# Three QR steps a tick, a QR tail in six places, and a shorter gap between the first two blocks

## The chip, the cores and the metric

The kernel runs on one core of a Trainium2 chip. The metric is the time on the device, in microseconds (us). The engines of a core work side by side, each through its own instructions in their order: TensorE (PE, with its weight loads PEld), VectorE (DVE), ScalarE (ACT), GpSimd (POOL) and SyncE (SP, which issues most of the DMAs).

## The reference

The input x has 32 sequences of 128 tokens with 144 channels. Four blocks follow each other, all conditioned on one vector a sequence. L0, L2 and L3 are transformer blocks with 16 heads of 9 channels; L0 normalises q and k, and L3 has four experts of which each token takes two. L1 is a rotation:

```python
U, _ = jnp.linalg.qr(P)                     # P: 144 x 64, one for all sequences
R = _rotation(cond, W, b)                   # expm of a skew 64 x 64 matrix a sequence
z = jnp.einsum('btn,nd->btd', x, U)
z_rot = jnp.einsum('btd,bde->bte', z, R)
x_rot = x + jnp.einsum('btd,nd->btn', z_rot - z, U)
```

Both the QR of P and the 32 matrix exponentials depend on the weights and the condition alone, not on x.

## The kernel before

All of x stays on the chip (`x_sb`). The three transformer blocks are called layers 0, 1 and 2 (L0, L2 and L3 of the reference). The kernel is one long loop over **ticks**. In a tick one sequence has its scores (`scores`, first half n = 0 and second half n = 1), the sequence before it has its scores once more, transposed, for the softmax weights, and the one before that has its attention output (`weigh`), its sums, its division and its projection. Sequence b of layer l begins at tick `first[l] + b`. Everything else is hung on to places of a tick. The places (called gaps in the code) are, in the order in which `fill` is called for them: a, e, t, first scores, stats, attention output, b0, b, den, (sums of layer 0), pre1, second scores, c, (division of layer 0), y1, y2, d, the largest scores, z. The instructions come out in exactly this order (`manual_schedule`), so each engine's queue is written out by hand: an instruction that waits holds up all that stand behind it on its engine. Banks of PSUM come from a pool of seven.

`GAP` is the number of ticks without a new sequence between layer 0 and layer 1: `first` is (0, 39, 71), so layer 0 has its scores in ticks 0 to 31 and layer 1 from tick 39. Layers 1 and 2 follow each other without a gap. The MLP of a group of four sequences of layer 0 is put 10 to 13 ticks behind the group's first tick; so groups 6 and 7 have theirs in ticks 34 to 41. The rotation of a group (`rotate_T`, `rotate_in`, `rotate`) is put 8 and 7 ticks ahead of the group's first tick in layer 1, and the layer norm and the q and k of layer 1 behind that.

Beside layer 0 the kernel prepares the rotation, by three generators that stop at each `yield`:

- `prep_qr`: 64 Householder steps of three pieces each (192 pieces, `qr_rest`), and then a tail of 18 pieces (a triangular inverse and U). In a step, piece one is a product on PE that spreads row j of `at` over all partitions (L322), ACT's square and its copy (L333, L335), and POOL's square root (L334). Piece two is five DVE instructions (L337 to L344), piece three two of them (L348, L349); the last one writes `at`, which the next step's product reads. The steps are one chain through four engines.
- `prep_expm`: 50 pieces: two layers' modulations and gates, the skew matrices (with two batches of weights by DMA), powers, two series, and four squarings in two pieces each. A squaring piece is 32 products of 64 x 64 on PE (L524) and two copies on ACT.
- `prep_rot`: eight pieces that make `rotU` out of U and the exponentials; behind it `load_late` frees the preparation's memory and loads the weights of layers 1 and 2.

`prepare_qr` gives out pieces of the QR: in ticks below 0 three a tick; from tick 0 six a tick, which is two steps (a: 1, t: 2, den: 1, y1: 1, y2: 1). When the steps are used up (tick 28), one piece of the tail is given out in every place of a tick, and then those of `prep_rot` in the same way: all in ticks 28 to 30. `prepare_expm` gives out one piece in b and one in z, up to tick 24. What is left at `last_prep` (tick 31, place d) is finished there; nothing is.

Of the kernel before, what the change touches and what calls it, by code (L numbers as in the profile page):

```python
# [65 lines left out]
def tile_kernel(ctx: ExitStack, tc: tile.TileContext, a: dict, out: bass.AP):  # L66
# [138 lines left out]
    def ring(shape, name, n, fill):  # L205
        bufs = []
        for i in range(n):
            t = const.tile(shape, F32, name=f"{name}{i}")
            fill(t)
            bufs.append(t)  # L210
        state = {"i": 0}

        def take():
            state["i"] += 1
            return bufs[(state["i"] - 1) % n]

        return take
# [93 lines left out]
    qr_rest = 3 * D  # L311
# [300 lines left out]
    def prep_rot(rotT):  # L612
        for b in range(0, NB2, 2):
            ps = bank([128, 2, C], f"ps_ru{b}")
            for i in range(2):
                for h in range(2):
                    rows = slice(h * D, (h + 1) * D)
                    nc.tensor.matmul(
                        ps[rows, i, :], rotT[rows, b + i, :], uT[rows, :], start=True, stop=True
                    )  # L620
            nc.scalar.copy(rotU[:, b : b + 2, :], ps)
            yield
# [10 lines left out]
    def ln_stats(pairs):  # L633

        n = len(pairs)
        name = "_".join(f"{kind}{s}" for s, kind in pairs)
        mv = small.tile([128, n, 2], F32, tag="mv", name=f"mv_{name}")
        for k, (s, kind) in reversed(list(enumerate(pairs))):
            bs = small.tile([128, 6], F32, tag="st", name=f"st_{kind}_{s}")
            nc.vector.bn_stats(bs, x_sb[:, of(s)[1], :])  # L640
            nc.vector.bn_aggr(mv[:, k, :], bs)  # L641
        rs = small.tile([128, 2, n], F32, tag="rs", name=f"rs_{name}")
        nc.gpsimd.tensor_scalar(rs[:, 0, :], mv[:, :, 1], 1.0, EPS, ALU.mult, ALU.add)  # L643
        nc.gpsimd.tensor_tensor(rs[:, 0, :], rs[:, 0, :], neghalf[:, :n], ALU.pow)
        nc.gpsimd.tensor_scalar(rs[:, 1, :], mv[:, :, 0], -1.0, 0.0, ALU.mult, ALU.add)
        for k, (s, kind) in enumerate(pairs):
            b = of(s)[1]
            minus, r = rs[:, 1, k : k + 1], rs[:, 0, k : k + 1]
            xh = work.tile([128, CM], F32, tag="xh", name=f"xh_{kind}_{s}", bufs=3)
            nc.gpsimd.tensor_scalar(xh, x_sb[:, b, :CM], minus, r, ALU.add, ALU.mult)  # L650
            xr = take_xr()
            nc.gpsimd.tensor_scalar(
                xr.rearrange("p (k c) -> p k c", k=4)[:, :, :CR],
                x_sb[:, b, CM:].unsqueeze(1).to_broadcast([128, 4, CR]),
                minus, r, ALU.add, ALU.mult,
            )
            st[s][f"xh_{kind}"], st[s][f"xr_{kind}"] = xh, xr
# [463 lines left out]
    late = L3 = None  # L1121
# [6 lines left out]
    def load_late():  # L1128
        nonlocal late, L3
        prep.close()  # L1130
        late = ctx.enter_context(tc.tile_pool(name="late", bufs=1))
        q = nc.sync
        PARAMS[1] = load_attn(late, "L2", q)
        load_mlp("L2", MLP_COLS)
        PARAMS[2] = L3 = Block()
        for k in ("wgate", "wgateR"):
            setattr(L3, k, load(late, f"L3_{k}", q))
        load_pair(0, late.tile([128, PAIR_COLS], F32, name="pair0"))
# [18 lines left out]
    prep_qr, prep_expm = prep_qr(), prep_expm()  # L1157
# [19 lines left out]
    def prepare_qr(tick, gap):  # L1177


        nonlocal prep_qr, prep_last, qr_rest  # L1180
        if late is not None:
            return
        if qr_rest:
            if tick < 0:
                pieces = {"e": 1, "stats": 2}
            else:

                pieces = {"a": 1, "t": 2, "den": 1, "y1": 1, "y2": 1}
            for _ in range(pieces.get(gap, 0)):
                next(prep_qr)  # L1190
                qr_rest -= 1
        elif prep_qr:
            if next(prep_qr, 0) == 0:
                prep_qr = None
        elif prep_last is None and not prep_expm:
            prep_last = prep_rot(rot_T[0])
        elif prep_last and next(prep_last, 0) == 0:
            load_late()

    def prepare_expm(tick, gap):  # L1200
        nonlocal prep_expm
        if prep_expm and (tick >= 0 and gap in ("b", "z") or (tick, gap) == (-2, "z")):
            said = next(prep_expm, 0)
            if said == 0:
                prep_expm = None
            elif said is not None:
                rot_T.append(said)


    GAP = 7  # L1210
    first = (0, B + GAP, 2 * B + GAP)
    at_tick = {first[l] + b: l * B + b for l in range(3) for b in range(B)}
    gaps = defaultdict(list)
    stats = defaultdict(list)
# [100 lines left out]

    def fill(tick, gap):
        prepare_qr(tick, gap)
        while (tick, gap) == (last_prep, "d") and late is None:
            prepare_qr(tick, gap)
            prepare_expm(tick, gap)  # L1320

        if gap == ("t" if tick < 0 else "e" if tick < first[1] else "stats") and tick in stats:
            ln_stats(stats.pop(tick))
        for f, args in gaps.pop((tick, gap), ()):
            f(*args)
        prepare_expm(tick, gap)

    last_prep = first[1] - 8
    for tick in range(-6, first[2] + B + 14):
        s0, s1, s2 = (at_tick.get(tick - k) for k in range(3))  # L1330
        for layer in range(3):
# [5 lines left out]
        while sums_later:  # L1337
            sums_later.pop()()
        fill(tick, "a")
        fill(tick, "e")  # L1340
        fill(tick, "t")
# [198 lines left out]
```

## Time and profile before

| what | us |
|---|---|
| median of 3 runs (lowest, highest) | 1370.38 (1369.37, 1375.61) |
| the profiled execution, its own time | 1370.79 |
| its span in the profile | 1368.0 |
| PE busy, PE's mean granted clock | 1296.2, 0.989 |
| start to tick 0's `q` (L822) | 51.1 |
| ticks 1 to 31 of layer 0 | 381.9 |
| ticks 32 to 39, between the layers | 46.2 |
| PE's idle time before QR products (L322), ended by DVE's `at` (L349) | 22.4, in 15 waits |

A tick is read here from one start of DVE's L822 (`q`) to the next, which occurs once a tick in which a sequence has its scores. "Busy" is the time in which at least one instruction of the engine was under way; PE's matmuls are pipelined and their ends are modelled. "x2 ... [1.91 <-DVE at L349]" behind a row says that the engine was idle for 1.91 us before it, and that DVE's write of `at` in line 349 ended the wait. PEclk is the share of its full clock that PE was granted.

### The profile page before, as it was taken

The page shows a single profiled execution, that of the slowest core. Times are in us where ns is not written, and L with a number is a line of the kernel's source. Part 1 is how long each engine was busy: PE and PEld are TensorE (multiplying, and loading weights), DVE is VectorE, ACT ScalarE, POOL GpSimd, SP SyncE. Part 2 cuts the span into 40 slices and gives each one's busy share as a digit, 9 for nine tenths or more (in the row PEclk, how much of TensorE's full clock was granted, in tenths as well). Part 3 has the DMA queues.
Part 4 walks back from the last instruction along what each step waited for, and adds up shares of the span by engine and source line. Part 5 has one row for each costly group of instructions (what it writes and reads, how often), then busy time and mean ns, then how long its engine had stood idle before and what let it go on. Part 6 is the DMA issues. An engine that isn't in the chain of part 4 may idle for free.

```text
span 1368.0 us, 35736 instructions
## 1 busy us (share of the span) xinstructions
PE 1296.2 (95%) x14210; PEld 951.4 (70%) x14210; DVE 825.7 (60%) x2632; ACT 812.3 (59%) x1800; POOL 639.6 (47%) x1663
## 2 busy tenths in 40 slices
PE   7999898999989988999999999999999999999998
PEld 5678687787767566677767676767676767676765
DVE  4698888866764357676666666646464545454322
ACT  2568776768746445776666767655555555554431
POOL 4667776655742523343443433626262626151622
PEclk9999999999999999999999999999999999999999
DMA  8200000000003000000110000200000000000000
GB/s 227 59 3 19 19 19 2 19 20 4 19 2 118 35 2 19 10 20 10 43 27 19 15 15 10 73 10 19 10 19 10 18 10 19 10 18 1 19 9 9
DMA packets 21608, 34.57 MB, mean 25 GB/s; under 512 B 2176, under 2 KB 12256, under 8 KB 21184
## 3 DMA queue, kind: packets, MB, share of 16 engines
q1 hardware_dynamic: 20848, 31.68, 7.8%
q8 instruction: 114, 1.87, 0.6%
q10 hardware_dynamic: 592, 0.59, 0.2%
q14 instruction: 54, 0.44, 0.1%
HBM read 29.79 MB, written 2.47 MB: 24 GB/s over the span
## 4 chain that ended last, share of the span: by engine, by line
PE 66%; DVE 8%; ACT 1%; issue 1%; POOLq 0%; POOL 0%; DVEq 0%
PE ps_h L682 19%; PE ps_f L1102 8%; PE ps_qk L682 6%; PE ps_s L858 5%; PE ps_o L885 5%; PE ps_w L858 5%; PE ps_f L975 4%; DVE nm L863 3%; PE ps_pj L949 3%; PE ps_v L682 2%; PE ps_f L1106 1%; PE ps_o L817 1%; DVE block L914 1%; DVE oT L916 1%; DVE block L910 1%
## 5 line engine op out<-in xcount | busy, mean ns | idle before, releaser
L863 DVE TENSOR_REDUCE nm<-ps_s 128x4 f32<-128x512 f32 x384 | 246.3, 682 | 88.1 <-PE ps_w L858 78.7
L870 ACT ACTIVATE pr<-ps_w 128x512 f32<-128x512 f32 x384 | 208.4, 595 | 143.6 <-PE ps_w L858 141.8
L858 PE MATMUL ps_w<-q,kT 32*128 32x128 f32 x3072 | 235.0, 284 | 1.6 <-DVE kT L736 1.6
L858 PE MATMUL ps_s<-kT,qT 32*128 32x256 f32 x1536 | 232.7, 408 | 0.1
L858 PEld LDWEIGHTS ps_w<-q,kT 32*128 32x128 f32 x3072 | 198.4, 188 | 13.3 <-issue 6.0
L969 ACT ACTIVATE hid<-ps_h 128x512 f32<-128x512 f32 (+1 forms) x224 | 119.3, 591 | 107.6 <-PE ps_h L682 107.3
L935 POOL TENSOR_TENSOR x_sb<-x_sb,res_a 128x144 f32<-128x144 f32 x96 | 46.9, 489 | 265.0 <-DVE res_a L938 264.4
L858 PEld LDWEIGHTS ps_s<-kT,qT 32*128 32x128 f32 x1536 | 136.3, 186 | 28.0 <-issue 9.0
L682 PE MATMUL ps_h<-hM_m,mlps 128*128 128x512 f32 x304 | 145.3, 611 | 0.0
L1110 DVE SCALAR_TENSOR_TENSOR acc<-ps_f,cw,acc 128x144 f32<-128x144 f32 x128 | 46.7, 366 | 158.6 <-PE ps_f L1106 72.3
L885 PE MATMUL ps_o<-pr,vaug 128*32 128x128 f32 x3072 | 105.0, 277 | 0.1
L885 PEld LDWEIGHTS ps_o<-pr,vaug 128*32 128x32 f32 x3072 | 78.8, 110 | 33.0 <-PE ps_w L858 18.5
L682 PEld LDWEIGHTS ps_h<-hM_m,mlps 128*128 128x128 f32 x304 | 54.2, 193 | 66.7 <-issue 65.8
L975 PE MATMUL ps_f<-mlps,hid 128*128 128x144 f32 x640 | 93.3, 293 | 0.0
L975 PEld LDWEIGHTS ps_f<-mlps,hid 128*128 128x128 f32 x640 | 82.4, 191 | 8.1 <-issue 5.1
L672 ACT ACTIVATE hM_m<-ps_hT_m,modM 128x128 f32<-128x128 f32 x96 | 44.6, 465 | 73.0 <-PE ps_hT_m L670 72.8
L643 POOL TENSOR_SCALAR rs_m_a<-mv_m_a 128x2 f32<-128x2 f32 x81 | 15.5, 191 | 137.2 <-DVE mv_m_a L641 109.7
L935 POOL TENSOR_TENSOR x_sb<-x_sb,res_m 128x144 f32<-128x144 f32 x64 | 32.6, 509 | 96.2 <-DVE res_m L938 96.2
L870 ACT ACT_TABLE_LOAD x55 | 70.6, 1283 | 5.6 <-PE ps_w L858 4.7
L1102 PEld LDWEIGHTS ps_f<-pair,hid 128*128 128x128 f32 x512 | 67.2, 191 | 8.4 <-issue 7.7
L1102 PEld LDWEIGHTS ps_f<-mlps,hid 128*128 128x128 f32 x512 | 67.2, 191 | 8.0 <-issue 6.9
L966 ACT ACT_TABLE_LOAD x56 | 71.8, 1283 | 1.0
(327 smaller groups left out, 2965.2 us busy)
## 6 DMA issues: line engine op xcount, KB each, us to landing
gates<-gates SPq DMA_DIRECT2D x48, 288.0 KB, 3.5
x_sb<-in_x SPq DMA_DIRECT2D x8, 288.0 KB, 8.7
out_x<-x_sb SPq DMA_DIRECT2D x8, 288.0 KB, 2.5
mlps<-in_L_mlp SPq DMA_DIRECT2D x2, 1000.0 KB, 6.7
wt<-in_W SPq DMA_DIRECT2D x6, 320.0 KB, 8.1
pair<-in_L_mlp SPq DMA_DIRECT2D x1, 1800.0 KB, 8.7
mlps<-in_L_mlp SPq DMA_DIRECT2D x1, 1800.0 KB, 8.5
mlps<-in_L_wmod SPq DMA_DIRECT2D x4, 290.0 KB, 4.7
```

The costliest lines, as they stand in the source:

```text
L672: nc.scalar.activation(gr[g][f"{k}_{kind}"][:, i, :], ps[:, k == "hR", :], AF.Identity, bias=m[:, sh, b : b + 1], scale=m[:, sc, b : b + 1],)
L682: nc.tensor.matmul(ps, x, y, start=k == 0, stop=k == 1)
L858: nc.tensor.matmul(o, x, y, start=True, stop=True)
L863: nc.vector.tensor_reduce(nmv[:, at0 : at0 + 2, ONE : ONE + 2], view.rearrange("p (r t k) -> p r t k", t=2, k=T), AX.X, ALU.max, negate=True,)
L870: nc.scalar.activation(pr[:, 4 * e : 4 * e + 4, :].rearrange("p s q -> p (s q)"), view, AF.Exp, scale=SCALE,)
L885: nc.tensor.matmul(po[rows4(j), t, :], v[:, 4 * j + 2 * t + r, :], prs[j // 2][:, 4 * (j % 2) + 2 * r + t, :], start=r == 0, stop=r == 1,)
L935: nc.gpsimd.tensor_tensor(x_sb[:, b, :], x_sb[:, b, :], t, ALU.add)
L966: nc.scalar.activation(t, half, AF.Gelu_apprx_tanh)
L969: nc.scalar.activation(hid[:n, i], ps[:n], AF.Gelu_apprx_tanh)
L975: nc.tensor.matmul(ps, hid[:, at0, i, :], w2[:, m, :], start=m == 0, stop=m == NFC - 1)
L1102: nc.tensor.matmul(ps[:, 0, :], hid[:, at0 + m, i, :], w2[:, at0 + m, :], start=m == 0, stop=m == 3)
L1110: nc.vector.scalar_tensor_tensor(acc, ps[:, 0, :], w, acc, ALU.mult, ALU.add)
```

## The change

Five things are edited.

1. In three ticks of four (`tick % 4 != 3`) three QR steps are given out instead of two: one more piece in stats and two in b. The piece that stood in den stands in pre1 in all ticks. The 192 pieces so end in tick 20.
2. The QR's tail and the pieces of `prep_rot` are given out in six places of a tick (stats, b, pre1, c, y1, z) instead of all: the tail in ticks 20 to 23, `prep_rot` in ticks 24 and 25, and `load_late` in tick 25.
3. In odd ticks `prep_expm` gets a third piece, in c. It ends in tick 19.
4. `GAP` is 2 instead of 7. Layer 1 begins at tick 34 and layer 2 at tick 66; there are five ticks fewer in all, and what is put by the layers' first ticks moves along: the rotation of group 0 comes to ticks 26 and 27, `load_L3` and the second pair of experts five ticks earlier.
5. The place at which the rest of the preparation would be finished is tick 27, c (`last_prep`). As before, nothing is left by then.

```diff
-                pieces = {"a": 1, "t": 2, "den": 1, "y1": 1, "y2": 1}
-            for _ in range(pieces.get(gap, 0)):
+                pieces = {"a": 1, "t": 2, "pre1": 1, "y1": 1, "y2": 1}
+                if tick % 4 != 3:
+                    pieces |= {"stats": 1, "b": 2}
+            for _ in range(min(pieces.get(gap, 0), qr_rest)):
                 next(prep_qr)
                 qr_rest -= 1
+        elif gap not in ("stats", "b", "pre1", "c", "y1", "z"):
+            return
         elif prep_qr:
...
-        if prep_expm and (tick >= 0 and gap in ("b", "z") or (tick, gap) == (-2, "z")):
+        gaps_ = ("b", "c", "z") if tick % 2 else ("b", "z")
+        if prep_expm and (tick >= 0 and gap in gaps_ or (tick, gap) == (-2, "z")):
...
-    GAP = 7
+    GAP = 2
...
-        while (tick, gap) == (last_prep, "d") and late is None:
+        while (tick, gap) == (last_prep, "c") and late is None:
             prepare_qr(tick, gap)
-            prepare_expm(tick, gap)
+            prepare_expm(tick, "b")
...
-    last_prep = first[1] - 8
+    last_prep = first[1] - 7
```

No instruction is added or taken away; PE has the same 6027 rows of matmuls in both programs.

## The prediction

> **What bounds the kernel now.** I read the page's busy row and 40 slices first, then the busy time by stage, then the order of the instructions inside one tick, and last the clock around PE's waits.
>
> ```profile
> PE 1296.2 (95%) x14210; PEld 951.4 (70%) x14210; DVE 825.7 (60%) x2632; ACT 812.3 (59%) x1800; POOL 639.6 (47%) x1663
> ...
> DVE  4698888866764357676666666646464545454322
> ```
>
> TensorE (PE) is nearly full everywhere, and its work is the same before and after: the change moves instructions and removes none. So a gain can only come out of PE's 72 us of idle time and the stretches in which its clock is lowered; a loss is new idle time. VectorE (DVE) is at 8 to 9 tenths in the first third alone, while the QR runs. The stages show where idle time lies (start:end, length, then PE, PEld, DVE, ACT, POOL busy, and PE's granted clock); each stage begins with one tick's `q` instruction (L822), so 51.1 is tick 0's, and the rows after it are ticks 1-20, 21-28, 29-30, 31, 32-39, 40-46 and 47-50:
>
> ```profile
> 51.10:286.70 235.60, 222.85 (x2966) 173.95 (x2960) 198.23 (x701) 166.41 (x461) 163.82 (x463) 0.97 0.07 19
> 286.70:388.30 101.60, 96.23 (x1375) 77.13 (x1372) 72.24 (x281) 74.67 (x200) 62.65 (x188) 1.00 0.04 14
> 388.30:423.60 35.30, 31.95 (x346) 23.41 (x347) 16.49 (x57) 15.93 (x36) 9.13 (x28) 0.90 0.01 2
> 423.60:433.00 9.40, 8.91 (x109) 6.07 (x109) 4.56 (x11) 6.67 (x15) 2.77 (x10) 1.00 0.86 289
> 433.00:479.20 46.20, 43.51 (x330) 29.03 (x329) 16.25 (x56) 22.73 (x50) 22.03 (x62) 0.99 0.14 55
> 479.20:548.30 69.10, 58.91 (x732) 42.30 (x731) 42.78 (x116) 35.28 (x73) 22.68 (x60) 0.96 0.04 10
> 548.30:588.50 40.20, 39.49 (x474) 28.40 (x473) 26.45 (x74) 27.50 (x54) 15.64 (x40) 1.00 0.03 9
> ```
>
> The seven nearly empty ticks between the layers (32-38) hold 43.5 us of PE work in 46.2 us: taking five of them away moves work elsewhere and frees little there. Ticks 40-46 have 10 us of idle, ticks 29-30 over 3 us and a clock of 0.90.
>
> Inside a tick with two QR steps (tick 7, 114.3 to 123.8) both engines are full. In the order of time:
>
> ```profile
> 116.59 1.08 PE L885 MATMUL ps_o<-pr,vaug 128*32 128x128 f32 x32
> ...
> 116.82 0.15 DVE L337 SCALAR_TENSOR_TENSOR ala<-qrr,qr 128x1 uint32<-128x1 uint32 x1
> ...
> 118.16 0.35 DVE L349 SCALAR_TENSOR_TENSOR at<-qrr,qr,at 128x123 f32<-128x123 f32 x1
> ...
> 118.43 1.28 DVE L863 TENSOR_REDUCE nm<-ps_s 128x4 f32<-128x512 f32 x2
> ...
> 119.04 0.48 PE L322 MATMUL ps_qr<-at,cst 128*128 128x124 f32 x2
> ...
> 120.84 1.29 DVE L863 TENSOR_REDUCE nm<-ps_s 128x4 f32<-128x512 f32 x2 [0.24 <-PE ps_s L858]
> ```
>
> PE ends the first scores and goes straight into the attention output (116.59), while DVE only then works on the first QR step (116.82 to 118.51: 1.69 us). The next QR product (L322) needs that step's `at`; it stands late, at 119.04, and waits for nothing.
>
> **The change part by part.** My sum is made against the profiled execution (1370.79 us, span 1368.0), 0.4 us over the median shown.
>
> *Three steps a tick.* 18 of 192 pieces are given out before tick 0. The other 174 need 29 ticks at six, and 21 ticks (0-20) at nine in three ticks of four: 16 ticks get a third step. Its product is put into the place "stats", which is ahead of the attention output in PE's order. At tick 7's times PE comes there at 116.59 and must wait for `at` until 118.51: **1.9 us of new PE idle**, with weigh, the values, the transposes and the second scores queued behind it. Follow DVE: `nm` to 119.71. The product ends at about 118.9; ACT's square and its accumulator (0.4 us after a hop of 0.6, as at 119.04 to 119.64) and POOL's power (0.55 us, behind the layer-norm chain that POOL ends at 119.57) give 120.1, so DVE idles 0.4. The second step runs 120.15 to 121.84. The third product, at "pre1", waits for that and takes 0.3: the second scores start at about 122.25 instead of 119.67. So 2.6 us a tick, of which 1.69 is DVE's own time: 16 x 2.6 = **+41.6**. Bounds: 16 x 0.8 = 13 if DVE's gaps (up to 2 us in ticks 2, 12, 13, 16, 18) take up half of its own time and the waits overlap, and 16 x 3.3 = 53 in ticks where POOL or ACT is later. In ticks with two steps the product moves past the two sums' transposes only: nothing, as it still starts 3 us before its DVE half.
>
> *PE's clock.* The page "TensorE: Matmul & The Clock Gate" of the Trainium skill (its section "HAM oscillation — how this bites in real kernels") says that PE's clock is lowered by idle gaps over about 3.4 us; by that a wait of 1.9 us is free of it. This trace says otherwise (the product's row, then two windows in the columns above):
>
> ```profile
> 162.59 0.45 PE L322 MATMUL ps_qr<-at,cst 128*128 128x116 f32 x2 [1.91 <-DVE at L349]
> ```
>
> ```profile
> 159.00:164.40 5.40, 3.49 (x68) 2.68 (x65) 4.87 (x20) 2.88 (x9) 4.67 (x13) 1.00 0.01 3
> 164.40:167.80 3.40, 3.40 (x11) 2.72 (x12) 3.26 (x12) 2.63 (x7) 2.91 (x9) 0.51 0.01 2
> ```
>
> A wait of 1.91 us for the very same instruction was followed by 3.4 us at half clock, and so were those of 1.95 us (76.88) and 2.80 us (213.29, 6.9 us). A stretch of 3.4 us at half clock makes 1.7 us of work late. By the rule this costs 0; by the row at most 16 x 1.7 = 27. I take 10 of the 16 (a wait may be split between two of the clock's stretches), half of it hidden by PE's other waits: 10 x 0.8 = **+8**.
>
> *Squarings.* A third exponential piece in odd ticks brings its 50 pieces to an end in tick 19 instead of 24. Of the eight squaring pieces (64 PE records, 12.29/6 = 2.05 us each), six lie after 286.7 now; afterwards all lie in ticks 15-18. 12.3 us of PE work enter ticks that DVE bounds. Placed between the scores, a piece is on the path; behind the second scores it lies beside 1.3 us of `nm`. Bounds 4 and 12; I take **+8**. The other pieces lie in ticks 0-19 before and after. The exponential's second matrix product (L437) now follows its own weights' load by less: it waited 0.93 us for the DMA before, and comes some 3 us earlier against a tick that is 2 us longer: **+2** (1 to 4).
>
> *Ticks 21-31* take 146.3 us and have 137.1 us of PE busy. From this go 12.3 for squarings, 16 QR products (6.1, from that line's 6.13 us for 16), and 2.8 of half-clock time at 389.6 to 396.5. To it come two groups' rotations and layer norms of the next layer: 1.0 + 0.7 + 0.9 (the starts at 437.13, 441.20, 455.98) twice and three transposes, 6.1. That is 122 us, with PE waits of about 4 left: the 18 QR-tail pieces stood in every place of tick 29 and waited for DVE at each; in six places of a tick other PE work lies between two. 126: **-20** (-25 to -13). load_late issues its nine DMAs on SP from tick 25 instead of 30; behind them wait the gate loads of tick 28 and later, at 3.5 us median to landing, and the weights are first read in tick 32: nothing. If SP's queue were held, the first loss would be tick 30's attention residual.
>
> *Ticks 32-46* (115.3 us) become 32-41. PE busy is 102.4, less 6.1 moved ahead and 3.4 of half-clock time at 478.4 and 512.5: 93. The following layer runs with 0.7 us idle in 40 (last row above), but the first block's MLP and the next layer's values now both start in one "stats" with five banks of seven, 1-2 us in two ticks. 97: **-18** (-22 to -13). What is late next there is PE itself.
>
> Sum: 41.6 + 8 + 8 + 2 - 20 - 18 = +21.6, that is 1392.4 for the profiled execution and **1392 us** as a median.
>
> **Rivals.**
> - *The clock decides* (slower, 0.17). Every new wait costs its full 1.7 us: +27 instead of +8, so 1411. For it: three waits of this instruction of 1.9 us and more, and three stretches at half clock. Against: DVE bounds these ticks, so part of PE's lateness costs nothing.
> - *VectorE's time alone counts* (no change, 0.13). The waits overlap with DVE's own pace: 16 x 1.7 = 27, squarings and load 10, no clock loss: 27 + 10 - 38 = -1, so 1370. For it: DVE busy is 8.49 of 9.5 us in tick 7. Against: PE is in order, and its wait stands ahead of what DVE needs next.
> - *The third step is nearly hidden* (faster, 0.20). With 0.8 us a tick (13) and 4 for squarings, 13 + 4 - 38 = -21: 1350. It decides below about 1.6 us a tick, where the two savings (38) outweigh 16 steps and some 12 us of the rest. For it: DVE's gaps of 2 us in several ticks. Against: DVE's own 1.69 us is already above that point.
>
> That the change doesn't do what it says I can rule out: in the changed order the QR's products stand between scores and output, and the QR ends in tick 20.
>
> **The numbers.** Forecast 0.50 (1380 to 1402), clock 0.17, no change 0.13, faster 0.20. From no change I can tell about 0.5%, 7 us. Slower by more: 0.50 + 0.17 + 0.03 of the third case = 0.70; within: 0.10; faster: 0.20. The range 1358 to 1410 leaves out about half of the fastest case and half of the clock's.
>
> **What would show it.** Right: L322 waits for DVE `at` L349 some 16 more times, near 1.9 us each, between first scores and attention output; ticks 0-20 take about 60 us more; more stretches at half clock before 350 us; ticks 21-31 near 126 us; the ticks to the steady layer near 97. Wrong: L322's waits stay at 22 us in all, or these ticks grow by under 35 us; or ticks 21-41 save over 45 us.

## The result, and the profile after

| | before | after |
|---|---|---|
| median (lowest, highest), us | 1372.99 (1369.37, 1382.34) | 1426.02 (1421.22, 1426.65) |
| span of the profiled execution, us | 1368.0 | 1423.9 |
| PE's mean granted clock | 0.989 | 0.967 |
| PE idle before QR products (L322), ended by DVE's `at` (L349) | 12.0, in 8 waits | 42.0, in 21 waits |

The changed kernel is slower: ratio 1.0375 [1.0341, 1.041]. Here and below, a ratio is to runs of the kernel before that were made beside it on the same chip (medians 1371 to 1374 us), and the brackets hold its 95% interval. The direction was forecast, the size was not: 1426 lies above the range (1358 to 1410).

The last row counts PE's own idle time. The 22.4 us in 15 waits given for the kernel before, and the 22 us of the prediction, add the idle time of the weight loads of the same products (10.4 us in 7 waits); counted so, the changed kernel has 64.0 in 35. The group of these products, before and after (count | busy, mean ns | idle before them, and what ended it):

```profile
L322 PE MATMUL ps_qr<-at,cst 128*128 128x145 f32 (+42 forms) x128 | 30.0, 319 | 13.5 <-DVE at L349 12.0 <-DMA at<-in_PT 0.6 <-ACT gsb L291 0.5
```

```profile
L322 PE MATMUL ps_qr<-at,cst 128*128 128x145 f32 (+42 forms) x128 | 32.0, 337 | 45.5 <-DVE at L349 42.0 <-ACT pr L870 2.0 <-DMA at<-in_PT 0.9
```

The page of the changed kernel, its busy row and three of its rows of 40 slices (tenths):

```profile
PE 1323.1 (93%) x14210; PEld 973.2 (68%) x14210; DVE 829.1 (58%) x2632; ACT 825.2 (58%) x1806; POOL 636.0 (45%) x1648
...
PE   6878788988999998899999999999999999999998
...
DVE  4586877655755545566766666745554545454422
...
PEclk9889888998999999999999999999999999999999
```

PE has the same work (14210 matmul records in both profiles; the 6027 rows given above stand in no view) and yet 27 us more of busy time; the clock row says why: 8 tenths in five of the first eight slices. And although VectorE is still the second busiest there, it has fallen from 8 or 9 tenths to between 5 and 8: neither engine is full any more. The stages (start:end, length; PE, PEld, DVE, ACT, POOL busy with counts; PE's clock), cut at the `q` of ticks 0, 20, 31 and of the next layer's eighth tick:

```profile
0.00:58.60 58.60, 43.48 (x347) 33.57 (x351) 27.77 (x134) 16.40 (x57) 28.68 (x96) 0.89 0.51 139
58.60:368.70 310.10, 262.30 (x3385) 205.79 (x3386) 221.05 (x821) 182.51 (x520) 170.29 (x478) 0.88 0.05 15
368.70:495.80 127.10, 124.33 (x1460) 93.90 (x1459) 75.28 (x235) 89.78 (x200) 71.30 (x222) 1.00 0.14 45
495.80:602.70 106.90, 95.90 (x1001) 68.39 (x1000) 55.42 (x157) 61.71 (x117) 35.97 (x93) 0.97 0.04 12
602.70:1423.90 821.20, 797.10 (x8028) 571.56 (x8026) 449.55 (x1289) 474.81 (x913) 329.73 (x759) 1.00 0.06 18
```

Before, these were 51.1, 235.6, 146.3, 115.3 and 819.6. Ticks 1 to 20 lose 74.5 us and are where the case is decided; the start loses 7.5, ticks 21 to 31 gain 19.3, the ticks between the layers only 8.4.

One tick shows both losses. PE in tick 10, with the start, the length, and in brackets the idle time ahead:

```profile
186.33 0.64 PE L858 MATMUL ps_w<-q,kT 32*128 32x128 f32 x4
189.48 0.74 PE L322 MATMUL ps_qr<-at,cst 128*128 128x110 f32 x2 [2.51 <-DVE at L349]
...
192.16 1.94 PE L885 MATMUL ps_o<-pr,vaug 128*32 128x128 f32 x32
194.03 3.52 PE L682 MATMUL ps_h<-hM_m,mlps 128*128 128x512 f32 x6
```

```profile
185.20:195.40 10.20, 7.69 (x66) 4.71 (x63) 6.64 (x27) 3.78 (x12) 6.14 (x15) 0.50 0.15 59
```

The third step's product waits behind the first scores, as forecast, but for 2.51 us and not 1.9. And everything around it is slow: the attention output (L885) takes 1.94 us where tick 7 of before took 1.08, and the second row says that PE ran at half clock for 10.2 us, not for 3.4.

### The profile page after: what moved, and what is told of

Same layout as the page of the kernel before. It is cut to its first block, busy times and chain, and to the rows that moved or that the text cites. A ratio compares the mean times of both kernels' runs of the same rounds, so it can differ in the third digit from the quotient of the medians.

```text
span 1423.9 us, 35720 instructions
## 1 busy us (share of the span) xinstructions
PE 1323.1 (93%) x14210; PEld 973.2 (68%) x14210; DVE 829.1 (58%) x2632; ACT 825.2 (58%) x1806; POOL 636.0 (45%) x1648
## 3 DMA queue, kind: packets, MB, share of 16 engines
q8 instruction: 114, 1.87, 0.5%
## 4 chain that ended last, share of the span: by engine, by line
PE 66%; DVE 7%; ACT 1%; issue 1%; POOL 0%; POOLq 0%; DVEq 0%
PE ps_h L682 18%; PE ps_f L1102 8%; PE ps_s L858 6%; PE ps_o L885 5%; PE ps_qk L682 5%; PE ps_w L858 5%; PE ps_f L975 4%; DVE nm L863 3%; PE ps_pj L949 3%; PE ps_v L682 2%; PE ps_f L1106 1%; PE ps_o L817 1%; DVE block L914 1%; DVE oT L916 1%; DVE block L910 1%
## 5 line engine op out<-in xcount | busy, mean ns | idle before, releaser
L858 PE MATMUL ps_s<-kT,qT 32*128 32x256 f32 x1536 | 235.8, 412 | 0.7 <-ACT kT L793 0.7
L969 ACT ACTIVATE hid<-ps_h 128x512 f32<-128x512 f32 (+1 forms) x224 | 119.6, 591 | 105.5 <-PE ps_h L682 105.2
L885 PE MATMUL ps_o<-pr,vaug 128*32 128x128 f32 x3072 | 109.5, 286 | 0.0
L885 PEld LDWEIGHTS ps_o<-pr,vaug 128*32 128x32 f32 x3072 | 81.8, 113 | 35.3 <-PE ps_w L858 18.2
L975 PEld LDWEIGHTS ps_f<-mlps,hid 128*128 128x128 f32 x640 | 84.8, 195 | 7.8 <-issue 4.7
L672 ACT ACTIVATE hM_m<-ps_hT_m,modM 128x128 f32<-128x128 f32 x96 | 44.5, 463 | 71.9 <-PE ps_hT_m L670 71.7
L322 PE MATMUL ps_qr<-at,cst 128*128 128x145 f32 (+42 forms) x128 | 32.0, 337 | 45.5 <-DVE at L349 42.0
```

Of the source, the lines that this page charges most:

```text
L672: nc.scalar.activation(gr[g][f"{k}_{kind}"][:, i, :], ps[:, k == "hR", :], AF.Identity, bias=m[:, sh, b : b + 1], scale=m[:, sc, b : b + 1],)
L858: nc.tensor.matmul(o, x, y, start=True, stop=True)
L885: nc.tensor.matmul(po[rows4(j), t, :], v[:, 4 * j + 2 * t + r, :], prs[j // 2][:, 4 * (j % 2) + 2 * r + t, :], start=r == 0, stop=r == 1,)
L969: nc.scalar.activation(hid[:n, i], ps[:n], AF.Gelu_apprx_tanh)
L975: nc.tensor.matmul(ps, hid[:, at0, i, :], w2[:, m, :], start=m == 0, stop=m == NFC - 1)
```

## The experiments

The theory at the start: the clock is the term that was too small. The rivals: the third step's own place, the shorter gap, the third exponential piece. Stages in us; "half" is the time at half clock between the `q` of ticks 0 and 20.

| kernel | ticks 1-20 | half | ticks 21-31 | to the next layer's 8th tick |
|---|---|---|---|---|
| before | 235.6 | 13.7 | 146.3 | 115.3 |
| after | 310.1 | 71.9 | 127.0 | 106.9 |
| e1_busy | 290.7 | 17.1 | 127.0 | 105.4 |
| e2_late | 303.1 | 59.5 | 127.1 | 103.9 |
| e3_gap7 | 310.8 | 71.7 | 123.6 | 113.8 |
| e4_expm2 | 288.8 | 54.6 | 141.5 | 105.3 |
| e6_busy_expm2 | 274.2 | 13.7 | 141.5 | 105.5 |
| e5_two_steps | 255.5 | 17.1 | 123.1 | 124.3 |
| e7_two_expm2 | 234.2 | 6.8 | 136.7 | 125.5 |
| e11_third_from_21 | 258.2 | 25.7 | 147.3 | 120.7 |

**PE kept busy in the wait (e1_busy).** Two products of 128 x 512 that nobody reads stand ahead of the third step's product.

```diff
+    def keep_busy(tick):
+        ps = bank([128, 512], f"ps_busy{tick}")
+        for _ in range(2):
+            nc.tensor.matmul(ps, ident, cst[:, :512], start=True, stop=True)
...
                 if tick % 4 != 3:
                     pieces |= {"stats": 1, "b": 2}
+                    if gap == "stats":
+                        keep_busy(tick)
```

> The changed kernel, but ahead of each third step's product PE runs two 128x512 products that nobody reads[...], in the time in which it waits for VectorE anyway. Theory (the lowered clock is what the prediction took too small: 85 us at half clock in ticks 0 to 20, of which half is work made late): the stretches at half clock before 360 us shrink to under 40 us in all, and the time falls by 15 to 30 us, to 1396 to 1411. Rival (the waits themselves and VectorE's order are the price, the low clock is hidden behind them): the time stays at 1420 to 1432.

Measured: 1402.19 (1400.91 to 1402.74), ratio 1.0195 [1.0161, 1.0229]: 23.8 us less than after, with more work on PE. Tick 10 of this kernel:

```profile
175.15 0.44 PE L858 MATMUL ps_w<-q,kT 32*128 32x128 f32 x4
175.52 1.98 PE L1180 MATMUL ps_busy<-cst 128*128 128x512 f32 x4
177.43 0.44 PE L322 MATMUL ps_qr<-at,cst 128*128 128x110 f32 x2
...
178.87 1.08 PE L885 MATMUL ps_o<-pr,vaug 128*32 128x128 f32 x32
```

The product of the QR still starts 2.3 us behind the last scores' start, but the unread work (1.98 us) has taken the wait's place, and the attention output is back at 1.08 us. The whole stage:

```profile
54.90:345.60 290.70, 269.86 (x3437) 200.34 (x3430) 220.18 (x822) 181.91 (x518) 170.99 (x478) 0.97 0.06 16
```

The clock is 0.97 instead of 0.88, and the stage 19.4 us shorter. The clock theory stands. The remaining 29 us over before need another cause.

**The third step later in the tick (e2_late).**

```diff
-                    pieces |= {"stats": 1, "b": 2}
+                    pieces |= {"den": 1, "pre1": 2, "c": 1}
```

> The changed kernel with the same nine pieces in the same ticks, but the second step's product in den (behind the attention output, the values and the transposes), its VectorE pieces in pre1, and the third step's product in c. Theory (the product ahead of the attention output waits 1.9 us and the waits lower the clock): PE's waits for at at L322 fall from 64 us to under 35 us, the time at half clock before 360 us to under 45 us, the time to 1385 to 1402. Rival (VectorE's own time for the third step and the squarings are the price, wherever the product stands): over 1412.

Measured: 1409.02 (1405.32 to 1414.03), ratio 1.0242 [1.0195, 1.0289]: between the two. The group of PE's L322 in this kernel (in after it had 45.5 us of idle time, 42.0 of it ended by `at`):

```profile
L322 PE MATMUL ps_qr<-at,cst 128*128 128x145 f32 (+42 forms) x128 | 32.0, 337 | 46.1 <-DVE at L349 44.5 <-DMA at<-in_PT 0.9 <-ACT gsb L291 0.5
```

The wait has gone to the new place, whole (3.1 to 4.0 us in ticks 8, 9, 12 and 13, at c). Ticks 1 to 20 are 7.0 us shorter than in after, with 12.4 us less of half clock. So the wait is not a matter of where in the tick the product stands: at both places a third round through PE, ACT, POOL and VectorE did not fit between the other two.

**The gap alone (e3_gap7).**

```diff
-    GAP = 2
+    GAP = 7
```

> The changed kernel with the gap of seven ticks as before. Theory (the shorter gap moves PE work and saves little): 3 to 9 us slower than the changed kernel, 1429 to 1435. Rival (the shorter gap is itself a loss, since the ticks of the next layer now hold the MLP of the first): faster than the changed kernel, under 1422.

Measured: 1428.96 (two runs), ratio 1.0392 [1.0348, 1.0437]. Without the shorter gap the kernel is about 3 us slower, which the two intervals leave open (after: 1.0341 to 1.041); in the profiles the ticks between the layers and the seven behind them take 6.9 us more, ticks 21 to 31 take 3.4 less.

**Without the third exponential piece (e4_expm2), and that together with the busy wait (e6_busy_expm2).**

```diff
-        gaps_ = ("b", "c", "z") if tick % 2 else ("b", "z")
+        gaps_ = ("b", "z")
```

> The changed kernel without the third exponential piece in odd ticks, so that the squarings stand in ticks 19 to 23 again. Theory (squarings in ticks with three QR steps cost 8 us): 1414 to 1421. Rival (they fill PE's waits there and cost nothing): 1423 to 1432.

> The changed kernel with the two unread products ahead of each third step's product, and without the third exponential piece in odd ticks. Theory (the low clock and the squarings in ticks that VectorE bounds are two separate losses, 24 us and 9 us): 1389 to 1397. Rival (they are one loss, both removed by a full clock): 1399 to 1404.

Measured: e4 1417.23 (two runs), ratio 1.0307 [1.0263, 1.0351], 9 us less than after; e6 1398.76 (two runs), ratio 1.018 [1.0128, 1.0231], only 3.4 us less than e1. In e6 the piece is worth little, because the loss in one stage comes back in the next: without it ticks 1 to 20 are 16.5 us shorter (290.7 to 274.2) and ticks 21 to 31 are 14.5 longer. The two savings do not add up (23.8 and 8.8 apart, 27.3 together); 1398.76 lies just under the range of the second expectation's rival, and above that of my theory.

**Without the third step (e5_two_steps), and also without the third exponential piece (e7_two_expm2).** The QR then ends in tick 28, so that the gap has to be 8. In e7 only the tail's six places and the gap are left of the change.

```diff
-                if tick % 4 != 3:
-                    pieces |= {"stats": 1, "b": 2}
...
-    GAP = 2
+    GAP = 8
```

> The changed kernel without the third step: two QR steps in every tick from 0 to 28, all else as changed, but a gap of eight ticks, which the QR's later end needs. Theory (the third step with its waits carries the whole loss, the other edits save a little or nothing): 1364 to 1375. Rival (the third exponential piece or the moved places carry a good part of the loss): over 1378.

> Two QR steps in every tick and two exponential pieces, a gap of eight ticks: of the change only the six places for the tail are left (and pre1 for den). Theory (in six places the tail no longer waits at each piece; ticks 29 and 30 had 35.3 us with 3.3 us idle and 6.9 us at half clock, and one more nearly empty tick costs under 1 us): 1362 to 1370, faster than the kernel before. Rival (the tail's waits only move with its pieces): 1371 to 1377.

Measured: e5 1379.74 (ten runs), ratio 1.0027 [1.0003, 1.0052], 46 of the 53 us gone, but above what my theory allowed and in its rival's range (over 1378); e7 1373.2 (twelve runs), ratio 0.9997 [0.9971, 1.0023], as its rival had it. Ticks 21 to 31 take 9.6 us less than before, and the ticks behind them 10.2 more. Most of that is work that has only moved: the products of `rotU` (L618) and the first group's rotation now lie behind tick 31, and PE's busy time falls from 137.1 to 130.8 us ahead of that point and rises from 102.4 to 110.3 behind it. Between e7 and e6 stands the third step at nearly full clock (with the gap). Ticks 1 to 20 of e6, then of e7:

```profile
54.10:328.30 274.20, 255.09 (x3054) 188.42 (x3048) 218.77 (x821) 174.81 (x506) 168.18 (x478) 0.98 0.06 16
```

```profile
56.70:290.90 234.20, 222.47 (x2976) 173.74 (x2976) 198.13 (x702) 167.43 (x463) 164.30 (x463) 0.99 0.07 19
```

40.0 us for 15 third steps, **2.67 each**. VectorE's busy time grows by 20.6, that is 1.37 each; for the other half VectorE itself is idle.

**Is it VectorE's fullness, or the round itself? (e11_third_from_21).** In e5, whose QR steps of ticks 21 to 28 seemed free (123.1 us with them, 127.0 in after without any), the third step is given only from tick 21, where VectorE is busy 8.0 to 8.9 us in ticks of 10.2 to 11.6. Ticks 21, 22, 24 and 25 get a third step; in tick 26 the last two steps stand in the first and the third step's places.

```diff
+                if tick > 20 and tick % 4 != 3:
+                    pieces |= {"stats": 1, "b": 2}
```

> Two steps a tick up to tick 20 and three in three ticks of four only from tick 21, where no third exponential piece and no squaring is left, with a gap of 8 ticks. My theory, that a step costs what it does because VectorE is full in ticks 1 to 20, and next to nothing in ticks 21 to 28, whose QR steps were free at two a tick: the few third steps cost at most 1 us each, and the time is at most 1384. The rival, that a third step waits for the chain of engines wherever it stands, and so costs 2.7 us and its share of clock anywhere: 1390-1396.

Measured: 1402.66 (1396.42 to 1405.42), ratio 1.0212 [1.0173, 1.025]. My theory falls, and the rival's price was still too low: these five ticks are 23 us longer than in e5, and so is the kernel's time. Two ticks of it (22 and 25), then PE and VectorE in the second:

```profile
319.90:334.10 14.20, 11.21 (x121) 7.63 (x120) 9.71 (x42) 9.97 (x26) 8.25 (x25) 1.00 0.15 43
...
360.50:376.60 16.10, 13.71 (x137) 12.29 (x136) 10.26 (x44) 7.37 (x25) 8.99 (x26) 0.79 0.00 1
```

```profile
361.93 0.39 PE L858 MATMUL ps_w<-q,kT 32*128 32x128 f32 x4
364.71 0.69 PE L322 MATMUL ps_qr<-at,cst 128*128 128x85 f32 x2 [2.39 <-DVE at L349]
365.33 1.94 PE L885 MATMUL ps_o<-pr,vaug 128*32 128x128 f32 x32
```

```profile
362.91 0.14 DVE L337 SCALAR_TENSOR_TENSOR ala<-qrr,qr 128x1 uint32<-128x1 uint32 x1
...
364.23 0.33 DVE L349 SCALAR_TENSOR_TENSOR at<-qrr,qr,at 128x84 f32<-128x84 f32 x1
...
370.01 0.31 DVE L938 TENSOR_TENSOR res_m<-ps_f,gates 128x144 f32<-128x144 f32 x1 [1.88 <-PE ps_f L975]
```

VectorE has 6 us of idle time in this tick, and PE waits 2.4 us all the same: the second step's DVE half stands behind the statistics, residuals and norms that VectorE works off until 362.9, and PE stands with nothing else to do between its scores and that step's end. Ticks 21 and 22, at full clock, are 2.8 and 2.9 us longer than in e5 (10.3 and 11.4), about the price found above, and without unread products; tick 25 at clock 0.79 is 5.9 longer (10.3), tick 26, where the tail's first pieces come too, 7.1 (11.4). So a third step costs its wait here too, and the clock on top.

**The ticks between the layers (e10_mlp_in_c).** In after they saved 8.4 us where I had said 18. PE's group of the transposed maxima (L817) in them, of after:

```profile
L817 PE MATMUL ps_o<-cst,nm 128*128 128x128 f32 x6 | 1.9, 318 | 7.3 <-DVE nm L863 7.3
...
L817 PE MATMUL ps_nm<-cst,nm 128*128 128x128 f32 x2 | 0.6, 300 | 2.6 <-DVE nm L863 2.6
```

That is 9.9 us of idle time: nothing lies between the second scores and the transposes that need VectorE's maxima of them. So the MLP's first halves of the last two groups are put there.

```diff
-                put2(t0 + 10, "stats", "b", mlp1, g, 0, (0, 1, 2), True)
-                put2(t0 + 11, "d", "d", mlp1, g, 3, (3, SHARED), False)
+                m1, m2 = (("c", "c"),) * 2 if n >= 6 else (("stats", "b"), ("d", "d"))
+                put2(t0 + 10, *m1, mlp1, g, 0, (0, 1, 2), True)
+                put2(t0 + 11, *m2, mlp1, g, 3, (3, SHARED), n >= 6)
```

> The changed kernel, with the first halves of the MLP of groups 6 and 7 of the first block put into place c (ahead of the largest scores) instead of stats, b and d. My theory, that the ticks between the blocks save 10 us less than I said because nothing lies between the second scores and the transposes of their maxima, which wait 1 to 2 us for DVE there: ticks 32 to 41 take 98-101 us instead of 106.9, and the time is 1418-1422. The rival, that PE's banks or the weights' own chain set it: 105-109 us, and 1424-1428.

Measured: 1412.31 (two runs), ratio 1.0275 [1.0224, 1.0326]. The same stage and group:

```profile
487.90:585.60 97.70, 92.71 (x1001) 66.42 (x1001) 55.14 (x157) 60.75 (x117) 36.04 (x93) 0.98 0.04 14
```

```profile
L817 PE MATMUL ps_o<-cst,nm 128*128 128x128 f32 x6 | 1.8, 300 | 3.9 <-DVE nm L863 3.9
...
L817 PE MATMUL ps_nm<-cst,nm 128*128 128x128 f32 x2 | 0.5, 272 | 0.0
```

The stage takes 97.7, a little less than I had expected of it: of the 9.2 us saved, 6.0 are this group's idle time (9.9 to 3.9), and the other 3.2 are less of PE busy time. The time fell by 13.7, of which the stage is 9.2. In the profiled executions the start and ticks 1 to 20 are shorter too, by 4.9 and 2.9, with the same instructions: such differences come from one execution to the next (below).

**Unread work in waits of a two-step tick (e8_two_busy, e9_busy_3_11_15)**, to see whether the clock's term is worth anything to e7.

```diff
+                if gap == "pre1" and tick in (3, 11, 15):
+                    keep_busy(tick)
```

This is e9, with one product; e8 had two, and in ticks 2, 10 and 14. The waits that I meant lie one tick later: e8 is a miss of mine, and its three ticks only grew by 1.2 to 1.6 us. Of the three stretches named for e9, only the one at 220 us follows its wait directly: e7's waits of 1.5 and 1.25 us, at 83.5 and 169.2, were followed by full clock.

> The kernel of two steps, two exponential pieces and a gap of eight, with two unread 128x512 products ahead of the second QR product in ticks 2, 10 and 14, where it waited 1.9 to 2.8 us before and half clock followed. Theory (a wait of 1.9 us lowers the clock in this kernel, and work that fills the wait keeps it): 3 to 6 us faster than the same kernel without them. Rival (the products delay PE by as much as the clock gains): within 2 us of it.

> Two steps and two exponential pieces a tick as in the run before (1373.2), with one unread product of 128 x 512 ahead of the QR product in pre1 of ticks 3, 11 and 15 alone. Those are the ticks in which that product waited 1.5, 1.25 and 2.15 us and a stretch at half clock followed (at 90, 220 and 336 us). My theory, that a wait of over 1.2 us itself brings half clock and that unread work in it takes this away: the half-clock time before tick 20 falls by about 7 us or more and the time by 1 to 4, to 1369-1372. The rival, that at two steps a tick PE has slack enough for it not to matter: within 1 us of 1373.

Measured: e8 1375.67, ratio 1.001 [0.9982, 1.0037]; e9 1371.53, ratio 0.9983 [0.9963, 1.0004], twelve runs each. In e9's profile no half clock is left between the `q` of ticks 0 and 20, and the stage takes 231.8. But the next kernel has the same ticks and 12.2 us of half clock in them (235.6). So e9 stays inconclusive: what is left to save at two steps a tick is within what one execution differs from the next.

**A version to beat both (e12_mlp_later).** e9, with the MLP of the last two groups six ticks later, in c.

```diff
+                late_by = 6 if n >= 6 else 0
...
+                put2(t0 + late_by + 10, *m1, mlp1, g, 0, (0, 1, 2), True)
+                put2(t0 + late_by + 11, *m2, mlp1, g, 3, (3, SHARED), n >= 6)
```

> The last two-step version (1371.5), with the MLP of groups 6 and 7 of the first block put six ticks later and into place c: from the empty ticks 34 to 41 into ticks 40 to 47, the first of the next layer, in which the largest scores' transposes wait 11 us in all for VectorE. My theory, that these waits are time that PE can use: the ticks from 31 to the eighth of the next layer take 114-119 us instead of 125, and the time is 1361-1367, faster than the kernel before. The rival, that moving them only moves idle time (the rotation's copies in the emptied ticks, VectorE in the filled ones): 1370-1375.

Measured: 1378.14 (nine runs), ratio 1.004 [1.0013, 1.0067]. The rival's mechanism was right, and worse than it said. The empty ticks and the next layer's first seven, of e9 and then of e12:

```profile
419.90:478.60 58.70, 54.37 (x421) 35.82 (x420) 16.82 (x58) 27.89 (x62) 23.47 (x67) 1.00 0.24 84
478.60:545.20 66.60, 55.69 (x713) 41.69 (x712) 42.78 (x116) 34.40 (x71) 22.72 (x61) 0.95 0.05 10
```

```profile
430.10:491.30 61.20, 50.97 (x343) 31.15 (x343) 15.28 (x53) 23.74 (x52) 21.63 (x66) 0.78 0.21 76
491.30:561.50 70.20, 66.11 (x781) 47.39 (x780) 43.74 (x120) 46.06 (x88) 24.14 (x61) 1.00 0.03 10
```

The filled ticks take up the MLP for 3.6 us more, as meant. But the emptied ones get no shorter: PE now waits for the rotation and the layer norm there, and the clock falls to 0.78. One such wait:

```profile
456.22 0.33 PE L669 MATMUL ps_hT_m<-cst,xh_m 128*128 128x128 f32 x1 [3.11 <-POOL xh_m L650]
```

The work that was taken out had been the cover of a chain. No version here beats the kernel before by more than its interval.

## Why the prediction was wrong

In spans, the change was to cost 21.6 us and cost 55.9. The steps of the sum, against what the runs showed (for ticks 1 to 20 along e7, e6, e1 and after, which differ there by one part each; e7 itself is 1.4 us shorter there than before):

| step | said | measured | miss |
|---|---|---|---|
| third step, 15 ticks, at full clock | +39 | +40.0 (e6 - e7), less 1.4 | -0.4 |
| third exponential piece (squarings, load of the second matrix's weights) | +10 | +16.5 (e1 - e6) | +6.5 |
| PE's clock | +8 | +19.4 (after - e1) | **+11.4** |
| start and tick 0's third step | +2.6 | +7.5 | +4.9 |
| ticks 21 to 31 | -20 | -19.3 | +0.7 |
| the ticks after them | -18 | -8.4 | **+9.6** |
| the rest | 0 | +1.6 | +1.6 |

- **The third step** was right in its place and its price: 2.6 said, 2.67 measured. Its wait was said to be near 1.9 us; in after ten of the sixteen waits are 1.87 to 1.99 and six are 2.2 to 3.5. That the price came out so close is in part luck: VectorE's own time is 1.37 of it and not 1.69, and e11 shows that the price comes also where VectorE has time to spare.
- **The clock is the first step that failed**: "I take 10 of the 16 ..., half of it hidden by PE's other waits". The count was good: 11 of the 16 third-step waits in after were followed by half clock or lay in it. But the stretches were not all 3.4 us long; seven of these waits have one of 6.8 to 13.7. Between the `q` of ticks 0 and 20 there are 71.9 us of half clock, 54.8 more than in e1, which make 27 us of work late; 19.4 of it came out in the time. So some seven tenths came out and not half; my reading is that at half clock the QR's product and the next scores are late too, and so what VectorE waits for. The rival's 27 us for this term was the better number. Its 1411 missed for the other terms.
- **Which waits are followed by half clock** depends on when they fall. In each of the 14 traces, all changes of the clock lie whole multiples of 3.413 us apart (after's first stretches from tick 1 on begin at 79.38, 96.44, 106.68 and 120.34: 5, 3 and 4 multiples between them). Of PE's waits of 1.85 to 2.45 us at full clock behind tick 0, over all traces, the 39 that had at least 1.85 us inside one such window were all followed by half clock; of the 46 with under 1.6 us in any window five were. Two waits of 2.39 us in e11, the first cut by a window's border into 1.16 and 1.23 (tick 21), the second with 2.07 in one window (tick 25):

```profile
306.36:309.78 3.42, 2.26 (x35) 1.89 (x32) 2.88 (x15) 2.27 (x8) 2.77 (x8) 1.00 0.02 5
309.78:313.19 3.41, 2.19 (x40) 1.92 (x41) 2.68 (x11) 0.87 (x5) 2.61 (x7) 1.00 0.00 0
...
360.98:364.39 3.41, 1.34 (x27) 0.98 (x24) 2.79 (x16) 2.25 (x7) 2.79 (x8) 1.00 0.02 5
364.39:367.80 3.41, 3.09 (x36) 2.50 (x37) 2.44 (x10) 0.83 (x4) 1.81 (x5) 0.50 0.00 0
```

So the prediction's reason for 10 of 16, that a wait may be split, holds.

- **The rule of the Trainium skill** that I weighed ("TensorE: Matmul & The Clock Gate", section "HAM oscillation — how this bites in real kernels": idle gaps over about 3.4 us) would have made this term nothing; the runs make it 24 us in the medians, of waits of 1.9 to 3.5 us. The same page's "Part 1: The HAM clock gate" says that the window of activity is 3413 ns long and runs freely; the windows above, 3.413 us long and with borders that lie differently in each trace, agree with that.
- **The third exponential piece** came to 16.5, and its parts can be told from the ticks of e1 and e6. Ticks 16 to 20, with the squarings, are 9.5 us longer in e1, near the 8 said. Ticks 1 to 15 are 7.0 longer, where the sum had 2 for the load of weights: that wait does not occur (no product of L437 waits for a DMA in after or e1). So the term put at nothing, "The other pieces lie in ticks 0-19 before and after", failed: brought forward they cost time, with two QR steps a tick too (e5 is 10.3 us longer than e7 in ticks 1 to 15). The piece gave 14.5 back in ticks 21 to 31.
- **The split of these two depends on the order.** With the third exponential piece taken out first, the clock is 14.6 us (e4 - e6) and the piece 21.3 (after - e4). Together they are 35.9 where 18 was said; the clock's miss is 6.6 to 11.4, the piece's 6.5 to 11.3. In the medians the clock is the larger in either order (18.5 to 23.8 us, the piece 3.4 to 8.8), since the piece is in part given back.
- **Ticks 21 to 31** came out as worked out (126 said, 127.0 measured), at a clock of 1.00.
- **The ticks after them** failed at "What is late next there is PE itself". Late was VectorE's `nm`, with nothing put ahead of the transposes of it (9.9 us of PE's idle time). With the MLP there (e10) the stage is 97.7, against the 97 of the sum.
- **The start.** Six kernels (e5, e7, e8, e9, e11, e12) are the same up to tick 0's `q` and reach it after 56.0, 56.7, 47.9, 51.4, 48.5 and 55.8 us. Of the 7.5 us here some 3 are the third step in tick 0 (the seven kernels with it reach this point after 55.8 us on average, before and these six after 52.5); the rest can't be told from this spread. What makes the spread stays open: it isn't the clock alone, since e3 reached this point after 59.0 us with no half clock ahead of it, and after in 58.6 with 13.4.

So of 34 us missed, 18 are the clock's and the third exponential piece's in ticks 1 to 20 (in the table's order 11 and 6.5), 10 the missing cover between the layers, and 5 the start.

## What to carry to other kernels

Before putting one more round of a chain through several engines into a loop, ask how many rounds the tick's length holds; a round that didn't fit cost its wait in PE's queue here, at both places of the tick that were tried and also in ticks in which VectorE had 4 to 6 us to spare. Price every new wait of TensorE twice: its length, and the work behind it at half clock; unread products in the wait are a cheap test of the second part. Work that seems to lie idly in empty ticks may be the cover of a chain: look at what waits there before taking it out, and put some of it ahead of a transpose that waits for VectorE's result.

## What was not expected of the hardware

- Waits of 1.9 to 3.5 us on TensorE were followed by half clock for 3.4, 6.8 or 10.2 us, once for 13.7. Stretches join: after has 71.9 us of it in 310, and two unread products (1.98 us) in each wait bring that to 17.1 us.
- The clock changes at borders 3.413 us apart that the kernel does not set, and a wait's place between them matters: 39 of 39 waits with at least 1.85 us in one window were followed by half clock, and five of 46 with under 1.6.
- The same instructions meet the clock differently from one execution to the next: ahead of tick 0's `q`, e7 has none at half clock and e12, with the same instructions, 21.9 us; and twelve runs of e7 reach from 1365.9 to 1380.5 us. Differences under some 5 us need many runs here, whatever one profile says.
